# FFN weight transposes at other points of a head pair's loop, and the sums of k spread over two pairs of blocks

## The chip, the cores and the metric

The kernel runs on one core of a Trainium2 chip. The metric is the device time of a launch in microseconds; the time before is the median of three runs. All times below are microseconds unless marked ns. PE is the tensor engine, DVE the vector engine, ACT the scalar engine, POOL is GpSimd, SP the engine whose queue issues most loads.

## The reference

A graph layer of attention over 384 nodes and 1024 features with 16 heads of 64, then a feed-forward layer (FFN) whose weights and activations are rounded to 8 bits. Cut to what matters here:

```python
q = x @ wq.T + bq;  k = x @ wk.T + bk;  v = x @ wv.T + bv            # x: layernorm of the input, 384 x 1024
q2 = (q @ wiq.T + biq)  # and k2, v2 alike, split into 16 heads of 64
scores = einsum('hnd,hmd->hnm', q2, k2) * scale + mask[None]         # mask from the edge list
attn = softmax(scores, axis=-1)
out = einsum('hnm,hmd->hnd', attn, v2).reshape(N, OUT_F) @ wo.T + bo
x = x + out
scale = max(abs(w), axis=1, keepdims=True) / 127                     # each FFN weight, by rows
wq8 = clip(round(w / scale), -128, 127) * scale                      # w_gate, w_up: 352 x 1024, w_down: 1024 x 352
h = silu(xq @ w_gate8.T) * (xq @ w_up8.T)                            # xq: rounded layernorm of x
x = x + round8(h) @ w_down8.T
```

## The kernel before, in words

**The first stage (to about 161).** The projections q, k, v and the inner q projection go two blocks of 128 outputs at a time, by `project2` (L178): seven products of four fp32 matmuls (L189) in place of eight, by sums and differences of blocks. `left_sums` (L162) makes three sums of weight blocks on DVE (L169, L171, L173), and `right_sums` (L146) makes, for each input, eight subtractions (L157) of 128x384 elements, which give `t3`, `t1`, `t2` and `t4`, two subtractions for each. The second product needs the left sum `s2` (L171) and `t2`; the sixth needs a correction of the weights made on DVE inside the projection (L210). The evictions of a projection are L200, L206, L217, L218, L221 on DVE and L203, L213 on ACT.

After each product `project2` takes one step of a generator called `aside`, and what is left of `aside` after the seventh product runs behind it. The asides are the chunks of the edge mask (L412 and on, five steps for each group), the left sums of the next pair of blocks, and the right sums of the next input, taken in turn by `in_turn` (L228). In this stage the order on PE, SP, POOL, DVE and ACT is as written, except that the planner may slip in instructions of later stages on DVE and ACT.

**The second stage (about 161 to 334), the heads.** It loops over `NP` = 8 pairs of heads, p = 0 to 7. On PE, SP and POOL the order is written by hand; DVE and ACT are ordered by the planner, by its own simulated times. For each pair PE does:

- scores: `scores` (L588) computes four matmul tiles in PSUM (two row blocks, two heads; L600) after the first 2/16 of the fill, and two more at the end of the pair. DVE adds the mask and takes the row maximum (L606), ACT takes the exponential (L610), and DVE divides by the sums (L620).
- `weigh` (L623) of the pair before: three steps, each turning six 128x128 tiles of softmax weights into two PSUM tiles of the pool `ps_tp` (L630), copied out by ACT (L632); a fourth step multiplies by v (L638) and copies the result out on DVE (L642).
- fill: `inner_k` for the next two pairs where p is odd (7 products of 4 matmuls, 29 steps; evicted from the two buffers of `ps_mm`), `inner_v` where p is even (24 steps, L577, evicted at L583), and in pair 7 the first part of the output projection (12 steps, L648).
- prep: `ffn_weights` (L504), which goes through 14 units of FFN rows: 3 of w_gate and 3 of w_up (1024 wide), 8 of w_down (352 wide). Each `take(prep, 1)` turns the unit before on PE (eight bf16 transposes at L530 or three at L537), copies it out on ACT (L531, or L538 and L539), loads the row two units ahead on SP (L514), and quantises its own unit: maximum on DVE (L493), scale (L494), reciprocal (L496), int8 copy on ACT (L499), and the cast to bf16 on DVE (L501). 15 takes finish it.

`ps_tp` has two buffers, shared by the softmax weights and the FFN weights. `rows_p` holds three rows, `w8b` one buffer, `wqi` two; the cast of unit k can start when the transposes of unit k-2 have read their buffer. SP carries the loads of wik (`inner_k`), wiv (`inner_v`), the FFN rows, and at the start of pair 6 bo, x and the eight tiles of wo, in this written order; the pool of weight tiles has eight buffers.

In the loop, `fill_to(m)` advances the fill to m sixteenths. Before, at 6, 9 and 12 a step of `weigh` is followed by a `take(prep, 1)`: three in even pairs, one (at 6) in odd pairs:

```python
            fill_to(2)
            next(sc)
            for m in (6, 9, 12):
                fill_to(m)
                take(wg, 1)
                if p % 2 == 0 or m == 6:
                    take(prep, 1)
            run(fill)
```

**The rest (334 to the end)** is the output projection, the second layernorm and the FFN, with DVE and ACT again in written order.

Of the kernel before, what the change touches and what calls it, by code (L numbers as in the profile page):

```python
# [36 lines left out]
KC = F // P  # L37
# [19 lines left out]
def row_bcast(ap, n):  # L57
    return bass.AP(tensor=ap.tensor, offset=ap.offset, ap=[[0, P], [1, n]])
# [3 lines left out]
def gnn_ffn_kernel(ctx: ExitStack, tc: tile.TileContext, a: dict, out: bass.AP):  # L62
# [14 lines left out]
    def load_w(name, j):  # L77
        wt = w.tile([P, F], F32, name="wt")
        nc.sync.dma_start(wt, a[name][j])
        return wt  # L80
# [15 lines left out]
    turned = ctx.enter_context(tc.tile_pool(name="turned", bufs=1))  # L96
# [49 lines left out]
    def right_sums(src, pool, name, in_place=True):  # L146


        b11, b21, b12, b22 = src[:, :HK, :HN], src[:, HK:, :HN], src[:, :HK, HN:], src[:, HK:, HN:]
        new = pool.tile([P, 3 if in_place else 4, HK, HN], F32, name=name, bufs=1)  # L150
        t2, t3, t4 = (new[:, j] for j in range(3))
        t1 = b12 if in_place else new[:, 3]

        def steps():
            for o, i0, i1 in ((t3, b22, b12), (t1, b12, b11), (t2, b22, t1), (t4, b21, t2)):
                for k in range(0, HK, 2):
                    nc.vector.tensor_sub(o[:, k : k + 2], i0[:, k : k + 2], i1[:, k : k + 2])  # L157
                    yield

        return (b11, b21, b22, t1, t2, t3, t4), steps()  # L160

    def left_sums(wa, wb, pool):  # L162

        half = HK * P
        s1 = pool.tile([P, half], F32, name="s1")
        s2 = pool.tile([P, half], F32, name="s2")

        def steps():
            nc.vector.tensor_add(s1, wb[:, :half], wb[:, half:])  # L169
            yield  # L170
            nc.vector.tensor_sub(s2, s1, wa[:, :half])  # L171
            yield
            nc.vector.tensor_sub(wb[:, :half], wa[:, :half], wb[:, :half])  # L173
            yield

        return (s1, s2), steps()

    def project2(wa, wb, sums, right, da, db, bias_a, bias_b, pool, name, aside=None):  # L178


        half = HK * P
        s1, s2 = sums
        b11, b21, b22, t1, t2, t3, t4 = right
        a1, a2, b1, b2 = da[:, :HN], da[:, HN:], db[:, :HN], db[:, HN:]

        def product(left, r):
            z = pool.tile([P, HN], F32, name=name)
            for k in range(HK):
                nc.tensor.matmul(  # L189
                    z, left[:, k * P : (k + 1) * P], r[:, k, :], start=(k == 0), stop=(k == HK - 1)  # L190
                )
                yield
            return z

        def other():
            if aside:
                aside()

        def add(dst, z, b, with_):
            nc.vector.scalar_tensor_tensor(dst, z, b, with_, op0=ALU.add, op1=ALU.add)  # L200

        z = yield from product(wa[:, :half], b11)
        nc.scalar.copy(a1, z)  # L203
        other()
        z = yield from product(s2, t2)
        nc.vector.tensor_add(b1, z, a1)  # L206
        other()
        z = yield from product(wa[:, half:], b21)
        add(a1, z, bias_a, a1)
        nc.vector.tensor_sub(wa[:, half:], wa[:, half:], s2)  # L210
        other()
        z = yield from product(s1, t1)
        nc.scalar.activation(b2, z, AF.Identity, bias=bias_b)  # L213
        add(a2, z, bias_a, b1)
        other()
        z = yield from product(wb[:, :half], t3)
        nc.vector.tensor_add(b1, z, b1)  # L217
        nc.vector.tensor_add(b2, b2, b1)  # L218
        other()
        z = yield from product(wa[:, half:], b22)  # L220
        nc.vector.tensor_add(a2, z, a2)  # L221
        other()
        z = yield from product(wb[:, half:], t4)
        add(b1, z, bias_b, b1)
        other()
        yield

    def in_turn(*steps):  # L228
        steps = list(steps)
        while steps:  # L230
            for s in list(steps):
                try:
                    yield next(s)
                except StopIteration:
                    steps.remove(s)

    def run(steps):
        for _ in steps:
            pass
# [4 lines left out]
    kT = act.tile([P, KC, N], F32, name="actT")  # L244
    vT = act.tile([P, KC, N], F32, name="actT")
    with ph1_stack:
# [97 lines left out]
        sums_next, steps = left_sums(*wq_next, ph1)  # L344
        run(steps)
        nc.vector.tensor_copy(bias, pt[:, : 5 * KC])
        x_right, steps = right_sums(xnT, ph1, "x_right", in_place=False)
# [97 lines left out]
        def bias_of(b):  # L445
            return bias[:, b * KC : (b + 1) * KC]
# [8 lines left out]
        for i, (name, o) in enumerate(todo[:-1]):  # L455
            (wa, wb), sums = wq_next, sums_next
            right, dst, cols = work[name]

            if name == "wq" and o == FIRST:
                aside = tables()  # L460
            elif name == "wiq" and o == KC - 2:
                k_right, aside = right_sums(kT, turned, "k_right")
            else:
                aside = islice(groups, GROUP + 1)
            wq_next = [load_w(todo[i + 1][0], todo[i + 1][1] + j) for j in range(2)]
            sums_next, steps = left_sums(*wq_next, turned if todo[i + 1][0] == "wik" else ph1)
            if name == "wv" and o == KC - 4:
                q_right, q_steps = right_sums(qT, ph1, "right")
                work["wiq"] = (q_right, q2, bias_of(3))
            if name == "wv" and o >= KC - 4:  # L470
                steps = in_turn(steps, islice(q_steps, 4))
            aside = in_turn(aside, steps)
            run(project2(
                wa, wb, sums, right, dst[:, o], dst[:, o + 1], cols[:, o : o + 1], cols[:, o + 1 : o + 2], ps_p, "p",
                lambda: next(aside, None),
            ))
            run(aside)
            if i == 0:
                nc.scalar.activation(sig, clip, AF.Sigmoid)
# [61 lines left out]
    with ExitStack() as ph:  # L541
        at = ph.enter_context(tc.tile_pool(name="at", bufs=4))
# [110 lines left out]
        def take(steps, n):  # L653
            for _ in range(n):
                if next(steps, "end") == "end":
                    return

        NP = H // 2
        prep = ffn_weights()
# [4 lines left out]
        for p in range(NP):  # L664
            if p % 2 == 0:
                k2 = k2_next
            sc = scores(q2[:, p], k2[:, p % 2])
            wg = weigh(p - 1, e_before) if p else iter(())
            if p == NP - 1:
                early = [(t, g, ps_mm.tile([P, 512], F32, name="mm")) for t, g in ((0, 0), (0, 1))]  # L670
                fill, n = (s for t, g, pm in early for s in out_group(wo, t, g, range(NP - 2), pm)), 2 * (NP - 2)
            elif p % 2:
                k2_next, fill = inner_k(p + 1)
                n = 7 * HK + 1
            else:
                fill, n = inner_v(p // 2), NT * KC
            if p == NP - 2:

                x = act.tile([P, NT, F], F32, name="actT")
                bo_b = w.tile([P, F], F32, name="wt")  # L680
                nc.sync.dma_start(bo_b, row_bcast(a["L0_gnn_bo"], F))
                for t in range(NT):
                    nc.sync.dma_start(x[:, t, :], a["x"][t * P : (t + 1) * P, :])
                for t in range(NT):
                    for g in range(2):
                        gs = slice(g * 512, (g + 1) * 512)
                        nc.vector.tensor_add(x[:, t, gs], x[:, t, gs], bo_b[:, gs])
                wo = [load_w("wo", k) for k in range(KC)]
            done = 0

            def fill_to(sixteenths):
                nonlocal done
                upto = n * sixteenths // 16
                take(fill, upto - done)
                done = upto

            fill_to(2)
            next(sc)
            for m in (6, 9, 12):
                fill_to(m)  # L700
                take(wg, 1)
                if p % 2 == 0 or m == 6:
                    take(prep, 1)
            run(fill)

            e_before = next(sc)
            take(wg, 1)
# [95 lines left out]
    with ExitStack() as ph:  # L803
# [109 lines left out]
        for t in range(NT):  # L913
            ts = slice(t * P, (t + 1) * P)
            for g in range(2):
# [10 lines left out]
                else:  # L926
                    o = ff.tile([P, 512], F32, name="o")
# [3 lines left out]
        for t, gs, y in last:  # L931
            o = ff.tile([P, 512], F32, name="o")
# [49 lines left out]
```

## Time and profile before

| what | value |
|---|---|
| median of 3 runs | 386.88 (386.22 to 388.01) |
| the profiled execution, its time | 387.15 |
| its span, first to last instruction | 385.4 |
| PE busy | 363.4 (94%) |
| DVE busy | 262.2 (68%) |
| ACT busy | 107.0 (28%) |
| granted PE clock, mean | 0.997 |

The span is the time from the first to the last instruction of the profiled execution. Its own time is 1.75 longer than its span. A busy share is an average over stages that differ: in the projections of q, k and v (24 to 142) PE has no idle time and DVE is busy 98.5 of 118; over the last 51 PE is busy 40 and DVE 39. A wait that ends on PE counts in full only where PE has nothing else to do. PE's ends are modelled, its starts are not.

### The profile page before, as it was taken

What the parts mean: (1) busy time and instruction counts of PE and PEld (TensorE: products, weight loads), DVE (VectorE), ACT (ScalarE), POOL (GpSimd) and SP (SyncE); (2) the same over time, 40 slices, a digit from 0 to 9 for tenths busy, and PEclk for the clock granted to TensorE, in tenths of its full rate; (3) what the DMA queues carried; (4) which work ended last, traced back from release to release, by engine and by line L of the source; (5) the groups of instructions that cost most, each with busy time, mean ns of one, the idle gap of its engine ahead of it and who ended that gap; (6) DMA issues with size and microseconds to landing.
All of it is one profiled execution on the core that took longest, in us unless ns stands there. A gap on an engine that the chain in (4) does not pass through costs nothing.

```text
span 385.4 us, 5844 instructions
## 1 busy us (share of the span) xinstructions
PE 363.4 (94%) x2100; PEld 299.4 (78%) x2101; DVE 262.2 (68%) x785; ACT 107.0 (28%) x256; POOL 79.5 (21%) x81
## 2 busy tenths in 40 slices
PE   7999999999999999899899999999989999998972
PEld 7899999999999999798686767768766445457660
DVE  5878888888789977995747376546662421298775
ACT  2252100000000100325545553555243423001430
POOL 6100354454445553830000000000000000000003
PEclk9999999999999999999999999999999999999998
DMA  7996333343433355274030504050573000000004
GB/s 236 376 378 229 112 111 109 113 129 111 116 120 124 134 168 201 78 230 134 30 129 1 167 0 128 8 177 2 199 292 85 26 0 2 0 0 1 2 1 163
DMA packets 17804, 44.50 MB, mean 115 GB/s; under 512 B 3262, under 2 KB 8400, under 8 KB 17392
## 3 DMA queue, kind: packets, MB, share of 16 engines
q1 hardware_dynamic: 15104, 39.46, 30.2%
q0 software_dynamic: 2672, 4.68, 4.0%
q8 instruction: 16, 0.26, 0.3%
q14 instruction: 12, 0.10, 0.1%
HBM read 41.91 MB, written 2.21 MB: 115 GB/s over the span
## 4 chain that ended last, share of the span: by engine, by line
PE 81%; DVE 11%; ACT 4%; DMA 1%; issue 1%; POOL 0%; POOLq 0%; ACTq 0%; DVEq 0%
PE p L189 35%; PE mm L577 11%; PE mm L189 8%; PE sc L600 4%; PE sc L638 3%; PE sc L648 3%; PE mm L648 3%; PE tp L630 3%; PE mm L303 3%; DVE e L620 2%; ACT e L610 2%; ACT eTs L632 1%; PE mm L791 1%; PE x L838 1%; DVE s L606 1%
## 5 line engine op out<-in xcount | busy, mean ns | idle before, releaser
L425 POOL DMA_INDIRECT mask_d<-value,place x51 | 64.2, 1259 | 65.3 <-DVE place L422 49.9
L189 PE MATMUL p<-actT,wt 128*128 128x192 f32 x360 | 66.0, 326 | 0.5 <-DVE wt L210 0.5
L189 PEld LDWEIGHTS p<-actT,wt 128*128 128x128 f32 x360 | 59.6, 190 | 0.8 <-DVE wt L210 0.8
L577 PE MATMUL mm<-wt,actT 128*128 128x256 f32 x192 | 45.9, 386 | 0.0
L610 ACT ACTIVATE e<-s,mn 128x384 f32<-128x384 f32 x48 | 29.1, 606 | 54.3 <-DVE mn L606 54.3
L577 PEld LDWEIGHTS mm<-wt,actT 128*128 128x128 f32 x192 | 35.0, 190 | 7.9 <-issue 2.2
L606 DVE CUSTOM_DVE_ANT_0 s<-sc,mask 128x384 f32<-128x384 f32 x48 | 24.4, 552 | 14.5 <-PE sc L600 13.8
L808 POOL MEMSET hT<- 128x384 f32 x1 | 0.4, 417 | 158.6 <-PE sc L638 158.6
L189 PE MATMUL p<-x_right,s 128*128 128x192 f32 x176 | 32.2, 326 | 0.0
L189 PE MATMUL p<-x_right,wt 128*128 128x192 f32 x176 | 32.2, 326 | 0.0
L189 PEld LDWEIGHTS p<-x_right,s 128*128 128x128 f32 x176 | 29.2, 190 | 0.0
L189 PEld LDWEIGHTS p<-x_right,wt 128*128 128x128 f32 x176 | 29.2, 190 | 0.0
L632 ACT COPY eTs<-tp 128x384 f32<-128x384 f32 x48 | 20.6, 480 | 26.3 <-PE tp L630 26.2
L412 DVE SCALAR_TENSOR_TENSOR junk<-key_b,key,later 128x384 f32<-128x384 f32 (+3 forms) x51 | 27.5, 540 | 0.0
L200 DVE SCALAR_TENSOR_TENSOR actT<-p,bias,actT 128x192 f32<-128x192 f32 x45 | 18.7, 416 | 8.4 <-PE p L189 5.1
L203 ACT COPY actT<-p 128x192 f32<-128x192 f32 x15 | 4.8, 318 | 66.1 <-PE p L189 66.1
L600 PE MATMUL sc<-k,actT 64*128 64x384 f32 x96 | 22.7, 522 | 0.2 <-DVE actT L642 0.2
L630 PEld LDWEIGHTS tp<-ident,e 128*128 128x128 f32 x144 | 17.2, 140 | 4.3 <-issue 2.6
L213 ACT ACTIVATE actT<-p,bias 128x192 f32<-128x192 f32 x15 | 6.3, 421 | 50.8 <-issue 28.7
L189 PE MATMUL mm<-actT,wt 128*128 128x192 f32 x96 | 20.1, 337 | 0.3 <-ACT k L203 0.3
L501 DVE CAST wqi<-w8b 128x352 bf16<-128x352 int8 (+2 forms) x14 | 6.9, 491 | 18.8 <-PE tp L537 9.8
L630 PE MATMUL tp<-ident,e 128*128 128x128 f32 x144 | 19.6, 273 | 0.0
(210 smaller groups left out, 593.9 us busy)
## 6 DMA issues: line engine op xcount, KB each, us to landing
wt<-in_wq_dram SPq DMA_DIRECT2D x8, 512.0 KB
wt<-in_wk_dram SPq DMA_DIRECT2D x8, 512.0 KB
wt<-in_wv_dram SPq DMA_DIRECT2D x8, 512.0 KB
wt<-in_wiq_dram SPq DMA_DIRECT2D x8, 512.0 KB
wt<-in_wik_dram SPq DMA_DIRECT2D x8, 512.0 KB
wt<-in_wiv_dram SPq DMA_DIRECT2D x8, 512.0 KB
wt<-in_wo_dram SPq DMA_DIRECT2D x8, 512.0 KB
actT<-in_x_dram SPq DMA_DIRECT2D x6, 512.0 KB
```

The costliest lines, as they stand in the source:

```text
L189: nc.tensor.matmul(z, left[:, k * P : (k + 1) * P], r[:, k, :], start=(k == 0), stop=(k == HK - 1))
L200: nc.vector.scalar_tensor_tensor(dst, z, b, with_, op0=ALU.add, op1=ALU.add)
L303: nc.tensor.matmul(pm_first[o][:, ts], wq_first[o][:, k * P : (k + 1) * P], xnT[:, k, ts], start=(k == 0), stop=(k == KC - 1),)
L412: nc.vector.scalar_tensor_tensor(junk[:, :left], keys[:, (c - k0) * P : (c - k0) * P + left], key[:, c : c + 1], later[:, :left], op0=ALU. ...
L425: ins = nc.gpsimd.indirect_dma_start(out=mask_d, out_offset=bass.IndirectOffsetOnAxis(ap=place[:, c : c + 1], axis=0), in_=value[:, c : c ...
L577: nc.tensor.matmul(pm, vT[:, k, t * P : (t + 1) * P], wt[k // HK][:, k0 : k0 + 256], start=(k == 0), stop=(k == KC - 1),)
L600: nc.tensor.matmul(ps[t, h], q2[hs, t * P : (t + 1) * P], k2[hs, :], start=True, stop=True)
L606: nc.vector.tensor_tensor_reduce(s, ps[t, h], mask[:, t, :], -SCALE, 3.0e38, op0=ALU.add, op1=ALU.min, accum_out=mn[h][:, t : t + 1],)
L610: nc.scalar.activation(e[h][:, t, :], s, AF.Exp, bias=mn[h][:, t : t + 1], scale=-1.0, accum_out=sm[h][:, t : t + 1],)
L630: nc.tensor.transpose(pt[:, t * P : (t + 1) * P], e[h][:, t, m * P : (m + 1) * P], ident)
L632: nc.scalar.copy(eT[h][m], pt)
L648: nc.tensor.matmul(pm, outT[:, k, t * P : (t + 1) * P], wo[k][:, gs], start=(k == 0), stop=(k == KC - 1))
```

## The change

Two edits. In the first stage, the subtractions of k's right sums begin one pair of blocks earlier: four are offered as asides in the inner q projection's third pair of blocks (`o == KC - 4`), the other four in its last (`o == KC - 2`), where all eight stood before. In the head loop, the steps of `ffn_weights` leave the places behind `take(wg, 1)` and go to `prepare`: after the fill's 2/16 and ahead of the scores in every pair, after 14/16 in pairs 2, 4, 5, 6 and 7, and after 6/16 and 12/16 in pair 0, ahead of `take(wg, 1)`, which has nothing to do there. The number of steps is 15 before and after; they end in pair 7, where they ended in pair 6.

```diff
             elif name == "wiq" and o == KC - 2:
-                k_right, aside = right_sums(kT, turned, "k_right")
+                aside = k_steps
             else:
                 aside = islice(groups, GROUP + 1)
...
             if name == "wv" and o >= KC - 4:
                 steps = in_turn(steps, islice(q_steps, 4))
+            if name == "wiq" and o == KC - 4:
+                k_right, k_steps = right_sums(kT, turned, "k_right")
+                steps = in_turn(steps, islice(k_steps, 4))
             aside = in_turn(aside, steps)
...
+            def prepare(at):
+                if at in ((2, 6, 12) if p == 0 else (2,) if p in (1, 3) else (2, 14)):
+                    take(prep, 1)
+
             fill_to(2)
+            prepare(2)
             next(sc)
             for m in (6, 9, 12):
                 fill_to(m)
+                prepare(m)
                 take(wg, 1)
-                if p % 2 == 0 or m == 6:
-                    take(prep, 1)
+            fill_to(14)
+            prepare(14)
             run(fill)
```

## The prediction

> **What bounds the kernel now.** I read the page first: TensorE (PE) is busy 94% of the span, and the chain that ended last is 81% PE, so only idle PE time, or work taken off PE, can shorten it.
>
> ```profile
> PE 363.4 (94%) x2100; PEld 299.4 (78%) x2101; DVE 262.2 (68%) x785; ACT 107.0 (28%) x256; POOL 79.5 (21%) x81
> PE 81%; DVE 11%; ACT 4%; DMA 1%; issue 1%; POOL 0%; POOLq 0%; ACTq 0%; DVEq 0%
> ```
>
> Then the waits of PE alone, longest first. The columns are: who waited for whom, us in total, times, longest.
>
> ```profile
> PE tp L537 <- ACT eTs L632: 3.4, 8, 1.5
> PE tp L530 <- ACT eTs L632: 2.1, 4, 1.2
> PE mm L189 <- DVE k_right L157: 1.1, 1, 1.1
> PE p L189 <- DVE wt L210: 0.5, 1, 0.5
> ```
>
> The first two are the FFN weights' transposes (L530, L537) waiting for the copy L632 of the softmax weights turned just before them; 14 units are turned, twelve of them behind softmax weights. The third is the inner k projection waiting for the sums of k.
>
> Third, the timeline, to size one such wait (start, duration): pair 4, then pair 7, where plain fill follows.
>
> ```profile
> 246.63 0.82 PE L630 MATMUL tp<-ident,e 128*128 128x128 f32 x6
> 247.22 0.86 ACT L632 COPY eTs<-tp 128x384 f32<-128x384 f32 x2 [0.32 <-PE tp L630]
> 247.75 0.33 PE L537 MATMUL tp<-ident_b,wqi 128*128 128x128 bf16 x3 [0.29 <-ACT eTs L632]
> 247.91 1.95 PE L577 MATMUL mm<-wt,actT 128*128 128x256 f32 x8
> ...
> 304.70 0.82 PE L630 MATMUL tp<-ident,e 128*128 128x128 f32 x6
> 305.35 1.88 PE L648 MATMUL mm<-wt,actT 128*128 128x512 f32 x4
> ```
>
> Six fp32 transposes take both buffers of `ps_tp`; the third tile has to wait until the first is copied out (copy start 247.22, mean 0.48). The next instruction can start 0.65 after them (304.70 to 305.35), but the weights' start after 1.12: 0.47 lost.
>
> Fourth, the timeline around the end of the q projection.
>
> ```profile
> 149.32 1.22 DVE L493 TENSOR_REDUCE wmx<-row 128x1 f32<-128x1024 f32 x1 [1.60 <-DMA row<-in_L_ffn_w_gate_dram]
> 158.48 1.57 PE L189 MATMUL p<-actT,wt 128*128 128x192 f32 x8 [0.52 <-DVE wt L210]
> 163.01 1.02 DVE L157 TENSOR_TENSOR k_right<-actT 128x384 f32<-128x384 f32 x2
> 163.71 1.54 PE L189 MATMUL mm<-k_right,s 128*128 128x192 f32 x8 [1.05 <-DVE k_right L157]
> ```
>
> The reader is to see that VectorE (DVE), not PE, sets the pace here: it has no gap from 149.32 to past 165, also because the planner put three reductions of FFN rows (L493, 1.2 each) into this stretch, the first held 1.60 by its load.
>
> **Part 1, the weights' transposes away from softmax weights.** The number of transposes, copies and quantisations stays: one step in each of 15 `take`s, only at other points. Removed is the wait. Start of the six transposes to start of the weights', less 0.65, in the order of time: 1.41, 0.46, 0.46, 0.40 | 0.41, 0.47, 0.47, 0.41 | 0.41, 1.65, 0.46, 0.46. Sum 7.5.
>
> [...] The profile's idle column gives only 3.4+2.1 = 5.5 for these twelve. [...] By the idle column the gain is 5.5, by starts 7.5. I take 7.5, because pair 7 shows the undelayed spacing directly; 5.5 stays as the low end.
>
> At the new points the buffers are free: at 2/16 the last softmax tile was turned a fifth of a pair, a score block and the weighted sum (2.09) ago; at 14/16 three or four fill matmuls stand between, 0.9 to 1.3, against a copy that ends 0.5 to 1.0 after its transposes. The quantised weights are there too: `wqi` has two buffers, so the cast of unit k waits for the transposes of unit k-2, and is needed two turns later, at least a pair's 17. So PE waits at the new points at about 0, at most 0.3 each.
>
> What the points at 2/16 do to others. They stand before the pair's four scores (L600), whose fourth PSUM tile needs the copy L642 of the pair before. Groups of eight score records take 1.56 undisturbed but 2.25 (pair 2), 2.10 (pair 5), 2.63 (pair 6), 2.33 (pair 7): 3.1 hidden in "busy". PE work moved ahead of them (0.45 for eight bf16 transposes, 0.16 for three, by starts) covers up to 0.45+3x0.16 = 0.9 of that, unless DVE's cast (0.34; 0.69 wide) gets before L642. I take -0.6 (ends -2.0, with pair 2's late load below gone, and +1.5, four or five casts ahead of L642).
>
> Behind the scores ScalarE (ACT) has, from that point, wdT copies 0.37+0.26 (wgT/wuT 1.01) and the int8 copy 0.59 (1.15). Queued behind them are the exponentials L610 and, in pairs 1, 3, 5, the eviction L203 on which the third product waits (0.32 at 228.74 already). The turned copies fit before the first exponential; an int8 copy may not. I put 0.2 on each of three pairs: +0.6 (0 to 2).
>
> In pairs 1 and 6 ACT copied softmax weights late (192.20 and 285.82), since DVE was late with scores; 1.41 and 1.65 came from that. With the weights gone, PE reaches the next softmax tile 1.6 to 1.8 later and finds the copy at 286.2, just in time; 0.3 to 1.1 of more DVE or ACT work ahead becomes a stall. +0.8 for both (0 to 2).
>
> SP's queue, past which row loads move: rows wait for a row buffer and everything behind them in SP waits too (90.4 in 11 waits, of which nothing reached PE). wik's pair for pair 3 stood behind row 8 and was issued at 195.62; DVE then waited 1.79 for it at 201.32. Now it stands behind row 7: earlier. That is a small gain within -0.6. The other way: row 13 moves behind bo, x and all of wo; the last two wo were issued at 294.15 and 296.2, so row 13 follows at their heels. A pair of 512 KB wik loads took 5.7 from issue at 195.62 to use, so row 13 lands perhaps 6 after, about 298 on a clock 4 to 6 earlier, when its reduction stands in DVE's queue. Its transposes are at 14/16 of pair 7, about 312 on the old clock: hidden, with some 5 to spare. If the reduction is queued ahead of pair 6's L620 or L642, up to 3 of stall follows; I cost it at 0 because the order of DVE is planned with that load in view, and keep 0 to 3. POOL's queue is passed by nothing.
>
> **Part 2, sums of k over two pairs of blocks.** Eight subtractions (0.47 each by starts) stand now behind q's last pair of blocks, four of them after its last product. Four go one pair of blocks earlier. The work of DVE is the same. Replayed by hand, with the trace's durations and the three reductions where they are: the first k subtraction takes the place of the second left sum (0.60) in the fourth slot, which goes to the sixth slot. That sum then ends at 154.1, where the next pair's second product could start at 152.60: 1.5 lost. The correction L210 ends at 160.16 and holds the sixth product by 0.85 more. The wait of 1.05 for k_right and the 0.52 for L210 are gone, but the second inner product starts at 164.1 against 163.71: +0.4. Were the reductions elsewhere, all waits of this stretch could go: 1.9 by starts. I take +0.4 (ends -1.9 and +1.5). The mask's last group keeps its slot, and pair 0 is long enough (first score block 172.97, next 184.72) to hide its load.
>
> **Sum**, against the profiled execution's own 387.15 (span 385.4, 1.75 around it): -7.5 -0.6 +0.6 +0.8 +0.4 = -6.3, 380.85. That execution stood 0.27 above the median, 386.88, so 380.6.
>
> **Rivals.**
>
> A, the forecast: waits go, small ones come. 379.0 to 382.5. For it: every removed wait has a named releaser; against: the DVE and ACT orders are planned anew. 0.64.
>
> B, DVE already sets the boundary between pairs, so that half the gain comes back as longer score groups and late evictions: the plus ends +1.5, +2, +2 above in part, 3 in all beyond the forecast, 383.0 to 385.0. For it: the 3.1 hidden in L600. Against: DVE is busy 63.1 of the 111 from 186 to 297, pairs 1 to 6 (busy time by stage). 0.15.
>
> C, slower: each of the seven pair starts (1 to 7) puts cast, reduction, turned copies and int8 copy in front of the scores' evictions. [...] At a pair's start the price is 0.34+0.52+0.63+0.59 = 2.1 if all is on the path. It decides from 7.5/7 = 1.1 for each pair; at 1.6 the sum is 7x1.6-7.5+0.4 = +4.1, 391.0. [...] 0.08.
>
> D, better: hidden score stalls and the k stretch both go (-2.0, -1.9 in part): 377.0 to 379.0. 0.11.
>
> That the points don't move the work off the softmax copies can be excluded: PE's order is written by hand.
>
> E, nothing: gain eaten to within 0.5% (about what a measurement of this kernel can tell from no change): between B and C, 0.02; with B's slow tail (0.03) it makes 0.05.
>
> **Numbers.** Over 0.5% faster means below 384.95: A, D and most of B, 0.87; same 0.05; slower 0.08. The range leaves out the lower 0.04 of D, the upper 0.04 of B, E and C, 0.18 in all: 377.8 to 384.2.
>
> **What would show it.** Right: the two waits of L530/L537 for eTs gone from PE's list; pairs 2 and 4 shorter by more than 1; L600's groups no longer than now; no wait for k_right, but one of 1 to 2 for a left sum (L171) and one for L210. Wrong: PE waiting for wqi, for L642 or for L203 by more than 3 in all; DVE waiting for a w_down row around pair 7's start; the first inner product's end later than now by over 1.5.

## The result, and the profile after

Seven runs of the changed kernel have a median of 384.3 (382.39 to 385.56), against 386.94 (386.22 to 388.99) for seven of the kernel before: ratio 0.9923, interval 0.9901 to 0.9946. It is faster by 2.6, where 6.3 were forecast, and 384.3 lies just above the range given (to 384.2). The changed kernel's profiled execution took 385.56 (span 383.8), at the upper end of its runs, so traces differ by only 1.6 in span. Lines of the changed kernel from L606 on stand three below those of the kernel before (L606 is L609, L632 is L635), from L642 to L645 alike; L493 to L542 likewise.

The page after: PE's share of the span, the granted clock in 40 slices, and the shares of the chain that ended last.

```profile
PE 364.5 (95%) x2101; PEld 301.2 (78%) x2101; DVE 261.1 (68%) x785; ACT 107.2 (28%) x256; POOL 74.6 (19%) x81
PEclk9999999999999999999989999999999999999996
PE 70%; DVE 14%; DMA 7%; ACT 5%; issue 2%; POOL 0%; SPq 0%; DVEq 0%; ACTq 0%
```

One slice inside the loop over the head pairs has an 8 in the clock row, and the last one a 6 (8 before); and the chain that ended last runs less through PE than before (81%) and more through loads and DVE. Next PE's waits (who for whom, us in total, times, longest):

```profile
PE mm L189 <- ACT k L203: 4.0, 3, 3.7
...
PE mm L189 <- DVE k L217: 1.0, 1, 1.0
PE p L189 <- DVE s L171: 0.7, 1, 0.7
...
PE tp L633 <- ACT eTs L635: 0.3, 1, 0.3
```

The weights' transposes no longer wait for eTs: that part of the change does what it says. At the head of the list stands a wait that was 0.3 before, for L203. In pair 4, shown before with a gap of 1.12, the fill now follows the six transposes after 0.66, and the three weight tiles start 0.17 ahead of the next fill:

```profile
249.58 0.82 PE L633 MATMUL tp<-ident,e 128*128 128x128 f32 x6
250.24 1.89 PE L580 MATMUL mm<-wt,actT 128*128 128x256 f32 x8
...
256.73 0.33 PE L540 MATMUL tp<-ident_b,wqi 128*128 128x128 bf16 x3
256.90 1.51 PE L580 MATMUL mm<-wt,actT 128*128 128x256 f32 x6
```

To see where the gain went I took, from both timelines of PE, the start of each pair's last scores, and from them the length of each pair:

| stretch | before | after | difference |
|---|---|---|---|
| start of the program to pair 0's last scores | 184.73 | 185.18 | +0.45 |
| pair 1 | 15.64 | 19.75 | +4.11 |
| pair 2 | 20.55 | 18.10 | -2.45 |
| pair 3 | 17.11 | 17.72 | +0.61 |
| pair 4 | 19.12 | 17.60 | -1.52 |
| pair 5 | 17.20 | 17.10 | -0.10 |
| pair 6 | 21.42 | 18.13 | -3.29 |
| pair 7 | 17.86 | 18.07 | +0.21 |
| from there to the end | 71.77 | 72.15 | +0.38 |

Pairs 2, 4 and 6 bring 7.26. Pair 1 takes 4.11 of it back, where 1.41 should have been gained. (The +0.38 of the last row goes with the clock and not with the change; the last section shows it.) Pair 1's PE timeline, from the last scores of pair 0 to its own:

```profile
185.18 0.92 PE L603 MATMUL sc<-k,actT 64*128 64x384 f32 x4
...
189.46 1.46 PE L189 MATMUL mm<-k_right,s 128*128 128x192 f32 x8
194.59 0.92 PE L189 MATMUL mm<-actT,wt 128*128 128x192 f32 x4 [3.67 <-ACT k L203]
...
197.46 2.33 PE L189 MATMUL mm<-actT,s 128*128 128x192 f32 x8
...
204.93 0.92 PE L603 MATMUL sc<-k,actT 64*128 64x384 f32 x4
```

`ps_mm` has two buffers, so the third product of `inner_k` needs the first one's buffer, which L203 on ACT empties. That product's last two matmuls (189.03, 0.59) were done at about 189.6. ACT at that time (here and below, ACT's reads of its accumulator, 0.19 each, are left out):

```profile
188.65 0.77 ACT L534 COPY wgT<-tp 128x768 bf16<-128x768 bf16 x1
190.97 0.62 ACT L613 ACTIVATE e<-s,mn 128x384 f32<-128x384 f32 x1 [1.54 <-DVE mn L609]
...
192.43 0.61 ACT L613 ACTIVATE e<-s,mn 128x384 f32<-128x384 f32 x1 [0.76 <-DVE mn L609]
193.04 0.60 ACT L613 ACTIVATE e<-s,mn 128x384 f32<-128x384 f32 x1
193.64 0.60 ACT L613 ACTIVATE e<-s,mn 128x384 f32<-128x384 f32 x1
194.24 0.29 ACT L203 COPY k<-mm 128x192 f32<-128x192 f32 x1
```

And before:

```profile
188.92 0.62 ACT L610 ACTIVATE e<-s,mn 128x384 f32<-128x384 f32 x1 [1.34 <-DVE mn L606]
189.53 0.30 ACT L203 COPY k<-mm 128x192 f32<-128x192 f32 x1
190.38 0.62 ACT L610 ACTIVATE e<-s,mn 128x384 f32<-128x384 f32 x1 [0.55 <-DVE mn L606]
```

In both kernels ACT has gaps here, since the exponentials wait for DVE's masked scores. Before, L203 stood behind one of pair 1's exponentials, which waited; after, behind all four, and for most of its gap of 1.54 and all of that of 0.76 ACT stood idle while L203's data was ready. The eviction comes 4.7 later (4.3 if both are counted from pair 0's last scores). The time of PE in four stretches (columns: stretch: length, then busy time and instructions of PE, PEld, DVE, ACT, POOL; granted clock, DMA share, GB/s) shows a second cost:

```profile
190.90:194.60 3.70, 0.03 (x2) 0.01 (x1) 3.09 (x13) 2.88 (x10) 0.00 (x0) 1.00 0.13 53
194.60:195.60 1.00, 1.00 (x7) 0.98 (x8) 0.33 (x1) 0.99 (x1) 0.00 (x0) 1.00 0.00 0
195.60:198.90 3.30, 3.30 (x15) 3.30 (x13) 1.36 (x4) 0.96 (x2) 0.00 (x0) 0.53 0.67 212
198.90:202.00 3.10, 3.10 (x22) 3.06 (x21) 2.42 (x6) 1.19 (x3) 0.00 (x0) 0.95 0.55 171
```

About 1.2 after PE went back to work its clock fell to half, from 195.8 to 199.2. PE was busy all of these 3.4, and at a clock of 0.50 they hold 1.7 of work at full speed: an estimated 1.7 lost. So pair 1 paid 3.67 for the wait, and the half clock on top.

### The profile page after: what moved, and what is told of

Its sections match the earlier page's. It is cut to its first block, busy times and chain, and to the rows that moved or that the text cites. A ratio compares the mean times of both kernels' runs of the same rounds, so it can differ in the third digit from the quotient of the medians.

```text
span 383.8 us, 5838 instructions
## 1 busy us (share of the span) xinstructions
PE 364.5 (95%) x2101; PEld 301.2 (78%) x2101; DVE 261.1 (68%) x785; ACT 107.2 (28%) x256; POOL 74.6 (19%) x81
## 4 chain that ended last, share of the span: by engine, by line
PE 70%; DVE 14%; DMA 7%; ACT 5%; issue 2%; POOL 0%; SPq 0%; DVEq 0%; ACTq 0%
PE p L189 33%; PE mm L580 7%; PE mm L189 6%; PE tp L633 4%; PE mm L651 3%; PE sc L651 3%; PE mm L303 3%; PE sc L641 3%; PE sc L603 3%; DMA row<-in_L_ffn_w_down_dram 2%; DMA wt<-in_wik_dram 2%; ACT e L613 2%; DVE e L623 2%; DVE s L609 1%; DMA row<-in_L_ffn_w_gate_dram 1%
## 5 line engine op out<-in xcount | busy, mean ns | idle before, releaser
L425 POOL DMA_INDIRECT mask_d<-value,place x51 | 59.3, 1162 | 62.1 <-DVE place L422 47.0
L609 DVE CUSTOM_DVE_ANT_0 s<-sc,mask 128x384 f32<-128x384 f32 x48 | 24.6, 550 | 13.1 <-PE sc L603 13.0
L635 ACT COPY eTs<-tp 128x384 f32<-128x384 f32 x48 | 20.7, 481 | 28.0 <-PE tp L633 27.9
L203 ACT COPY actT<-p 128x192 f32<-128x192 f32 x15 | 4.8, 320 | 66.1 <-PE p L189 66.1
L189 PEld LDWEIGHTS mm<-actT,wt 128*128 128x128 f32 x96 | 15.9, 196 | 8.3 <-ACT k L203 4.9
L603 PE MATMUL sc<-k,actT 64*128 64x384 f32 x96 | 21.7, 521 | 0.1
```

Source lines behind the costliest of these rows:

```text
L189: nc.tensor.matmul(z, left[:, k * P : (k + 1) * P], r[:, k, :], start=(k == 0), stop=(k == HK - 1))
L425: ins = nc.gpsimd.indirect_dma_start(out=mask_d, out_offset=bass.IndirectOffsetOnAxis(ap=place[:, c : c + 1], axis=0), in_=value[:, c : c ...
L603: nc.tensor.matmul(ps[t, h], q2[hs, t * P : (t + 1) * P], k2[hs, :], start=True, stop=True)
L609: nc.vector.tensor_tensor_reduce(s, ps[t, h], mask[:, t, :], -SCALE, 3.0e38, op0=ALU.add, op1=ALU.min, accum_out=mn[h][:, t : t + 1],)
L635: nc.scalar.copy(eT[h][m], pt)
```

## The experiments

Theory 1: the weights' step ahead of pair 1's scores makes the planner put L203 behind all four exponentials. Theory 2: the late L203 comes from elsewhere, from the k edit's other DVE order or from `inner_k`'s late weights. Theory 3: the gain of 7.5 was overrated. Theory 4, taken up from e5_fill3_pair1 on: more fill ahead of the scores is a gain in any kernel. All ratios are against runs of the kernel before on the same chip, with 95% intervals.

**Each half alone.** Weights' steps moved, k's sums as before:

```diff
-                aside = k_steps
+                k_right, aside = right_sums(kT, turned, "k_right")
...
-            if name == "wiq" and o == KC - 4:
-                k_right, k_steps = right_sums(kT, turned, "k_right")
-                steps = in_turn(steps, islice(k_steps, 4))
```

> Only the weights' transposes move; k's subtractions stand as before. [...] Theory 2 (late wik load, from the k edit): no wait for L203 over 0.5 us: 379.5 to 380.5. Theory 3 (the gain of 7.5 us was overrated): as the changed kernel, 384.

Measured: 385.01, ratio 0.9948 (0.9925 to 0.9971). PE's waits:

```profile
PE mm L189 <- ACT k L203: 4.2, 3, 3.8
```

The wait is there in full without the k edit, with the clock at 0.57 from 192.5 to 194 and at 0.50 from 194 to 196; pair 1 takes 19.59. Theory 1 had the wait at 1.5 to 2.5 and the time at 381 to 382.5; the wait is 3.8. The time alone would fit theory 3; the stretches don't, since pairs 2, 4 and 6 have their gain in full (18.10, 17.59 and 18.08, as in the changed kernel).

The other half, the k edit alone on the kernel before (its four changed lines, nothing else):

> Only k's subtractions move. Theory 1: ACT's order is that of before, no wait for L203; the k stretch itself gains about 1 us at the second inner product and gives it back inside the first inner projection: 386 to 387.5. Theory 2: wik's load for pair 1 is issued about 2.5 us late, DVE stands 2 us or more on it, and pair 0 or 1 is longer by 1 to 3 us: 387.5 to 389.5.

Measured: 387.26, ratio 1.0007 (0.9989 to 1.0024). PE's waits:

```profile
PE tp L540 <- ACT eTs L635: 3.4, 8, 1.5
PE tp L533 <- ACT eTs L635: 2.1, 4, 1.2
...
PE mm L189 <- ACT k L203: 0.3, 1, 0.3
```

The old waits for eTs are back, the one for L203 is not, and pair 1 is at 15.63. The k edit is not the cause, and by itself it is worth nothing that these runs can measure.

**The first product finished before the step.** With 3/16 of the fill instead of 2/16 in odd pairs, PE has done all of the first product when the weights' step and the scores come:

```diff
-            fill_to(2)
+            fill_to(3 if p % 2 else 2)
             prepare(2)
```

> The changed kernel, but odd pairs bring the fill to 3/16 (five steps) and not 2/16 (three) before the scores, so that the first inner product is complete and its eviction L203 stands ahead of the exponentials on ACT. Theory 1: the wait of 3.7 us and the half clock behind it go, PE gains about 5 us on a run that had both: 379.5 to 381. Theory 2: DVE is as late as in the changed kernel, so PE stalls elsewhere in pair 1 by 1.5 to 3 us: 381.5 to 383.

Measured: 377.66, ratio 0.977 (0.9747 to 0.9793). ACT in pair 1:

```profile
186.46 0.60 ACT L613 ACTIVATE e<-s,mn 128x384 f32<-128x384 f32 x1
...
187.06 0.30 ACT L203 COPY k<-mm 128x192 f32<-128x192 f32 x1
187.42 0.80 ACT L534 COPY wgT<-tp 128x768 bf16<-128x768 bf16 x1
...
190.39 0.62 ACT L613 ACTIVATE e<-s,mn 128x384 f32<-128x384 f32 x1 [0.26 <-DVE mn L609]
```

L203 now precedes the four exponentials and even the turned copy; no wait for it is left in PE's list, and pair 1 takes 14.53. It beats both kernels, and what was expected of it: 6.6 below the changed one by the medians, 5.9 by the two ratios. Its other gains come from pairs 3, 5 and 7 (16.37, 16.28, 17.48 against 17.72, 17.10, 18.07): every first group of eight scores takes 1.56 to 1.61.

**Earlier wik loads**, theory 2's other half: pair 1's `inner_k` gets its weights loaded right behind `inner_k(0)`.

```diff
+        wik_2 = [load_w("wik", 2 + j) for j in range(2)]
...
-                wa, wb = (load_w("wik", p + j) for j in range(2))
+                wa, wb = wik_2 if p == 2 else [load_w("wik", p + j) for j in range(2)]
```

> The changed kernel, but wik's two tiles for pair 1 are issued on SP ahead of pair 0's FFN rows; ACT's order in pair 1 stays as in the changed kernel. [...] Theory 2: the wait goes to under 0.5 us: 379.5 to 380.5.

Measured: 383.48, ratio 0.9901 (0.988 to 0.9922). PE in pair 1, then two stretches:

```profile
189.38 1.46 PE L189 MATMUL mm<-k_right,s 128*128 128x192 f32 x8
193.24 1.32 PE L189 MATMUL mm<-actT,wt 128*128 128x192 f32 x4 [2.40 <-ACT k L203]
```

```profile
190.80:193.30 2.50, 0.10 (x2) 0.06 (x1) 1.89 (x8) 2.21 (x8) 0.00 (x0) 1.00 0.00 0
193.30:196.90 3.60, 3.60 (x14) 3.51 (x15) 0.44 (x2) 1.90 (x3) 0.00 (x0) 0.54 0.44 123
```

The wait shrinks to 2.40 and stays, so the load is not its cause. DVE's own wait for wik, 2.37 in the changed kernel, is gone; the 1.27 by which PE's wait is shorter go with DVE's waits for two FFN rows between 172 and 190, 1.1 in all here and 2.5 there. (In e1_prep_only DVE waits for no wik in that time, but 2.7 for rows, and PE's wait is 3.8.) What is left is the place of L203 behind the four exponentials. The clock is at half behind it all the same (0.54 in the second stretch), and the time lies above the 380.5 to 382.5 that theory 1 gave, with a wait of 1.3 or more.

**One pair at a time.** Which part of the 6.6 is pair 1's? The 3/16 in that pair alone, and, separately, only pair 1's weights' step moved to 14/16:

```diff
-            fill_to(2)
+            fill_to(3 if p == 1 else 2)
```

> The changed kernel, with the fill at 3/16 before the scores in pair 1 alone. Theory 1 (ACT's order in pair 1 is the main loss): pair 1 becomes 14.5 us long as in the kernel with 3/16 in all odd pairs (14.53), and most of the 6.6 us by which that one beat the changed kernel is here: 379 to 380. Theory 4 (the gain of 3/16 is a general one, from later scores in every odd pair): 1.5 to 3 us only, 381.5 to 383.

```diff
-                if at in (... (2,) if p in (1, 3) else (2, 14)):
+                if at in (... (14,) if p == 1 else (2,) if p == 3 else (2, 14)):
```

> The changed kernel, with pair 1's step of the FFN weights at 14/16 and not at 2/16. The planner then has the eviction L203 behind one exponential, as in the kernel before. Theory 1: the wait falls to under 1 us, the clock stays whole, pair 1 is 14.5 to 15.5 us: 379.5 to 381. If the prep step's own work at 2/16 is not what made ACT late, the wait stays over 2 us and pair 1 over 17: 383 to 384.5.

Measured: 380.29, ratio 0.9834 (0.9814 to 0.9853), pair 1 at 15.17; and 379.98, ratio 0.9823 (0.9799 to 0.9846), pair 1 at 14.63. ACT in pair 1 of the second:

```profile
189.20 0.62 ACT L613 ACTIVATE e<-s,mn 128x384 f32<-128x384 f32 x1 [1.73 <-DVE mn L609]
...
189.82 0.30 ACT L203 COPY k<-mm 128x192 f32<-128x192 f32 x1
190.67 0.62 ACT L613 ACTIVATE e<-s,mn 128x384 f32<-128x384 f32 x1 [0.55 <-DVE mn L609]
```

With that one step elsewhere the order of ACT is the old one again, pair 1 is shorter by 5.12 (19.75 to 14.63), and the kernel stands 0.6 below the 380.6 forecast. (Of the first, 380.29 is a little more than the 379 to 380 expected, and its pair 1 has a new wait of 0.8 for L206 on DVE.) Theory 1 holds: this one step, at this one place, costs the missing part.

**The clock by itself.** PE kept at work through the wait, with 24 transposes of the identity, ahead of pair 1's third product, that nothing reads:

```diff
+            if p == 1:
+                take(fill, 8 - done)
+                done = 8
+                pt = ps_tp.tile([P, P], F32, name="tp")
+                for _ in range(24):
+                    nc.tensor.transpose(pt, ident, ident)
             for m in (6, 9, 12):
```

> The changed kernel, with 24 transposes of the identity (about 2.6 us) put on PE ahead of pair 1's third inner product, where PE stood idle for 3.7 us. Nothing else is done earlier. If the idle time alone is the loss: no change, 384 to 385. If the idle time also halved PE's clock for 3 us after it: the granted clock stays at 1.00 through pair 1, pair 1 is 17.5 to 18.2 us in place of 19.75, 382 to 383.

Measured: 383.0, ratio 0.9898 (0.9881 to 0.9916).

```profile
190.58 2.78 PE L713 MATMUL tp<-ident 128*128 128x128 f32 x24
193.54 0.92 PE L189 MATMUL mm<-actT,wt 128*128 128x192 f32 x4 [0.18 <-ACT k L203]
```

L203 is as late as ever behind its exponentials (it starts at 193.19), but PE works until just before the third product. The clock is at 1.00 from 185.2 to 203, and pair 1 takes 18.05 in place of 19.75. Not all of these 1.7 are the clock's. Up to the third product 0.87 is won, since a row came earlier (ACT's int8 copy at 184.13 rather than 185.26, and the exponentials after it). From the third product to the next pair's first scores it takes 9.51 against 10.34: 0.83 won, with new waits in it, for a row that DVE awaited for 2.24. e6_pair1_at14 shows that stretch without either: 9.08, less 0.45 for the eight transposes that it has there, 8.63. So the half clock cost the changed kernel 1.7 at most in this trace, and at least 0.8 of it is shown by this run; between the medians it is 1.3, earlier row included, and there the intervals overlap. That the transposes held the clock is not shown: the third product also starts earlier here, at 193.54 and not at 194.59, and the same start without them was not run.

**Is 3/16 simply better?** The same fill in the kernel before:

```diff
-            fill_to(2)
+            fill_to(3 if p % 2 else 2)
```

> The kernel before, with the fill at 3/16 before the scores in odd pairs. Control: without the moved weights the eviction L203 was never behind more than three exponentials, and its waits were 0.3 us (pair 3) and less. Theory 1: only those and part of the late score groups go, 1 to 2.5 us: 384.3 to 385.8. Theory 4: 5 us or more, 380 to 382.

Measured: 386.26, ratio 0.9969 (0.9956 to 0.9982): 0.8 faster, less than expected. The 6.6 of e3_fill3 is not a gain that the kernel before also had in it, and theory 4 falls.

**What is left to get.** Three kernels, each an edit shown above or two of them together: e3's without the k edit; e3's with e6's; and a sixteenth more of fill in every pair:

```diff
-            fill_to(2)
+            fill_to(4 if p % 2 else 3)
```

> The weights' transposes moved and 3/16 in odd pairs, k's subtractions as before. Tells what the k edit is worth with ACT's wait out of the way. If the k stretch is bound by DVE either way, as forecast: 377.5 to 378.5, no more than 0.6 us from the kernel with both (377.7). If the k edit is worth the 1 to 2 us of PE waits that it removes: 378.8 to 380.

> The changed kernel with both cures: 3/16 in odd pairs, and pair 1's weights at 14/16. If both act on the same wait, they don't add: 377 to 378.2. If what is left of pair 1's lateness (its eviction L206 and the softmax copies) is also from the prep step: 376 to 377.

> The changed kernel with the fill at 4/16 before the scores in odd pairs and 3/16 in even ones. The scores come 1 us later after the pair before, which gives DVE time for L642, but a later start for this pair's exponentials. If score groups still wait for L642: 376.5 to 377.5. If none is left: 377.5 to 378.5.

Measured: 378.38, ratio 0.9785 (0.9764 to 0.9805); 378.35, ratio 0.9782 (0.9755 to 0.981); 378.32, ratio 0.9771 (0.9758 to 0.9785). All three ratios lie in the interval of e3_fill3. The two cures of pair 1 don't add up, since each removes the same wait (with both, pair 1 waits 1.03 for L206 and takes 15.52), and more fill brings no more. The k edit is worth 0.7 by e9_prep_fill3 against e3_fill3 and by e1_prep_only against the changed kernel, both across chips, and -0.4 by e2_k_only against the kernel before: not resolved.

## Why the prediction was wrong, and where it was right

**The wrong step: +0.6 for ScalarE behind the scores.** "I put 0.2 on each of three pairs: +0.6 (0 to 2)". In pairs 3 and 5 the wait for L203 is 0.3 in all; in pair 1 it is 3.67, with up to 1.7 of half clock on top. The row the estimate was taken from, 0.32 at 228.74, was the price of L203 behind three exponentials that ran without a gap between them (226.57 to 228.39), so the number ahead of it is not what counts. I asked how long the moved copies are (0.77 here) and not how far the eviction can fall back in a queue that is planned anew: behind four exponentials, two of which waited for DVE. By e4_wik_early 2.40 of the 3.67 stay when DVE is early again. By e6_pair1_at14 the step costs 5.1 in pair 1 (from the last scores to the third product 9.41 against 5.55, from there on 10.34 against 9.08), where the text's upper end for three pairs was 2. The prediction itself had named a wait for L203 "by more than 3 in all" among the signs that would prove it wrong (it was 4.0), but gave it no price near the true one.

**The row that was weighed.** Rival C, a price at each pair's start, was put at 0.08. Against it stood two rows of the trace before: DVE's casts had waited 9.8 and 9.0 for PE in twelve places, and PE's list has no wait for a cast.

```profile
DVE wqi L501 <- PE tp L537: 9.8, 6, 1.8
...
DVE wqi L501 <- PE tp L530: 9.0, 6, 1.9
```

These rows tell of DVE's casts where long fill covers them. They don't tell of ACT at a pair's start, where an eviction with a single spare buffer stood in the line: in pair 1 ACT was idle for 1.54 ahead of an exponential, most of it with L203's data ready. Rival C still fell: it charged all seven starts, and one paid. Rival B's range, 383.0 to 385.0, holds the measured 384.3, but by luck: its mechanism, DVE setting every boundary, did not occur, since pairs 2, 4 and 6 kept their gains.

**No term for the clock.** The forecast counted a wait at its own length. The trace before showed PE idle for 1.25 at 191 and for 1.48 near 286 with the clock at 1.00, and for 2.04 at 372 likewise, so nothing in it warned.

**The removed waits: right.** In pairs 2, 4 and 6 the nine waits are 5.24 by starts, the longer score groups of pairs 2 and 6 another 0.69 and 1.07, and three steps fewer are turned in these pairs (0.45+0.16+0.16): 7.77 in all, of which 7.26 arrived. Pair by pair that is 2.46, 1.51 and 3.80, against 2.45, 1.52 and 3.29. By the idle column the nine waits are 3.7 and the whole is 6.2, with 0.96 for pair 4: too little, so the choice of starts was right.

**+0.8 for late copies in pairs 1 and 6: right in size, and in pair 6 in kind.** Pair 6 kept 0.5 of the above for itself, and the wait of 0.3 for eTs that is left in PE's list is its second softmax tile (287.09), as forecast. Pair 1, in e6_pair1_at14, is 1.01 shorter than before where 1.41 of wait was taken away: 0.4, but no wait for a copy stands there, so that half fits in size only.

**-0.6 for the score groups: right in sign, with another distribution.** The excess over 1.56 goes from 3.1 to 2.1, by 1.0. Pairs 2 and 6 lose theirs; pair 3 gains one, and its timeline shows how:

```profile
227.13 0.52 DVE L496 TENSOR_REDUCE wmx<-row 128x1 f32<-128x352 f32 x1 [0.43 <-DMA row<-in_L_ffn_w_down_dram]
...
227.48 2.59 PE L603 MATMUL sc<-k,actT 64*128 64x384 f32 x8
227.56 1.07 DVE L623 TENSOR_SCALAR e<-e,rs 128x384 f32<-128x384 f32 x3
...
228.55 0.55 DVE L645 COPY actT<-sc 128x384 f32<-128x384 f32 x1
```

A row's maximum, which waits 0.43 for its load, and the divisions stand ahead of the eviction L645 that the fourth score tile needs. I had feared the cast there; it was the reduction.

**+0.4 for k's sums: the steps were wrong, and the sum fits by luck.** "The second inner product starts at 164.1": it started at 162.57, 1.14 earlier than before. The wait for `s2` was 0.74 rather than 1.5 and none came for L210, since the reductions stood elsewhere. What was won went again in the inner projection that follows:

```profile
153.37 1.57 PE L189 MATMUL p<-right,s 128*128 128x192 f32 x8 [0.74 <-DVE s L171]
...
162.57 1.46 PE L189 MATMUL mm<-k_right,s 128*128 128x192 f32 x8
...
169.09 1.22 DVE L496 TENSOR_REDUCE wmx<-row 128x1 f32<-128x1024 f32 x1 [1.33 <-DMA row<-in_L_ffn_w_up_dram]
...
170.63 1.57 PE L189 MATMUL mm<-k_right,wt 128*128 128x192 f32 x8 [0.99 <-DVE k L217]
```

The last reduction waited 1.33 for its row, L217 stood behind it, and PE waited 0.99 for L217. The first scores came 0.45 later than before, 173.42 against 172.97. That is less than single traces differ by: these scores start at 172.54 to 173.42 in the eight kernels with this edit and 2/16 of fill in pair 0, and at 171.97 to 173.67 in the four without the edit. So the size of this term is not resolved.

**Row 13 behind wo at 0: right.** Its maximum ran at 298.84 without a wait.

**What stays open.** Why the planner put L203 last in pair 1 can't be read from a trace: its simulated times are not in it. A version that fixes ACT's order by hand was not tried.

## What to carry to other kernels

When a step is moved ahead of work whose evictions another engine does in planned order, look for the eviction with the fewest spare buffers and ask how far back it can fall: the price is everything that it may stand behind, with the waits of that work, not the length of what was moved. Finish the product that needs it before the moved step: one sixteenth more of fill turned 2.6 of gain into 9.2 (386.82 to 377.66). And lay out the result by stretches before explaining it: pairs 2, 4 and 6 together did about what was forecast, and one step in one pair took away more than half of the gain.

## What the runs showed of the hardware

A wait of PE can cost more than its length. In the changed kernel's trace the clock is at half from 195.80 to 199.21, behind the wait of 3.67, and from 373.30 to 376.71, behind one of 1.81 at 369.97. A stretch of the same length ahead of each, and the two themselves (columns as above):

```profile
192.38:195.79 3.41, 1.20 (x9) 1.18 (x10) 2.10 (x9) 3.16 (x8) 0.00 (x0) 1.00 0.00 0
195.79:199.21 3.42, 3.42 (x14) 3.42 (x13) 1.44 (x3) 0.96 (x2) 0.00 (x0) 0.50 0.69 215
369.88:373.30 3.42, 1.56 (x7) 0.60 (x7) 2.89 (x8) 1.12 (x2) 0.00 (x0) 1.00 0.00 0
373.30:376.71 3.41, 3.27 (x8) 1.17 (x8) 2.01 (x4) 0.00 (x0) 3.23 (x3) 0.50 0.20 77
```

Ahead of them PE was busy for 1.20 and 1.56. The next row is the 3.41 up to the end of the wait of 1.81:

```profile
368.37:371.78 3.41, 1.60 (x16) 1.37 (x14) 2.62 (x10) 1.29 (x3) 0.00 (x0) 1.00 0.00 0
```

And the kernel before, the 3.41 up to the end of its wait of 2.04 at 371.94, and the 3.41 behind it:

```profile
370.57:373.98 3.41, 1.38 (x13) 1.25 (x13) 2.72 (x10) 1.18 (x3) 0.00 (x0) 1.00 0.00 0
373.98:377.39 3.41, 3.03 (x13) 1.26 (x13) 2.90 (x6) 0.00 (x0) 1.94 (x2) 1.00 0.00 0
```

In the kernel before the wait is the longer one, and PE's work up to its end is less, 1.38 against 1.60; yet its clock stayed at 1.00. So neither the length of a wait nor PE's work in the 3.41 up to its end tells whether half clock follows. What decides is not shown by these runs.

The last stretch of the program shows the price once more. From pair 7's last scores to the end, the four traces whose clock row ends in a 6 (the changed kernel, e3_fill3, e8_before_fill3, e11_fill4) take 72.1 to 72.2, the other nine 71.7 to 71.8. So the 0.38 of the first table's last row goes with the half clock there and not with the change, which e8_before_fill3 does not have.
